# Gates, in_proj and ssm_out as 32x32 tiles in one block of a fused scan kernel

## The chip, the cores and the metric

The kernel runs on one NeuronCore of a Trainium2 chip. Its engines work side by side, each through its own list of instructions in order, and wait for one another by semaphores: TensorE (PE in the profile) multiplies matrices into PSUM, VectorE (DVE), ScalarE (ACT) and GpSimd (POOL) work element by element, SyncE (SP) issues DMAs. PSUM has eight banks, numbered 0 to 7 here, of 128 partitions by 512 float32. The metric is the device time of one launch in microseconds (us).

## The reference, cut to what matters

The input x is (4, 128, 96, 96) in float32. After a group norm it is read as four sequences of 9216 positions: along rows, rows reversed, along columns, columns reversed. Each goes through the same layer, and a matrix (fuse) joins the four results, which are added to x.

```python
t = _grouped1x1(x, in_proj_w, in_proj_b, 4)      # 4 groups: 128 -> 512 channels
u, gate = t[:, :256], t[:, 256:]
u = silu(u)
u = depthwise conv of u, 5 taps
s = ssm_in_w @ u                                 # 256 -> 32, as the next three
a = DMIN + (DMAX - DMIN) * sigmoid(ssm_delta_w @ u + b)
bb, cc = tanh(ssm_b_w @ u + b), tanh(ssm_c_w @ u + b)
prefix = cumsum(log(a))
hst = exp(prefix) * cumsum(bb * s * exp(-prefix))  # h = a*h + bb*s, step by step
u = u + ssm_out_w @ (cc * hst + ssm_d * s)       # 32 -> 256
u = _grouped1x1(u * sigmoid(gate), mix_w, mix_b, 4)
y = out_proj_w @ u                               # then fuse, over the four directions
```

All matrix products are float32.

## The kernel before

**Units and pairs.** mix, out_proj and fuse are multiplied into one matrix per direction ahead of the loop (`w_fin`). For each of the 4 images there are two phases, columns (V) and rows (H); a phase has 6 strips of 16 lines, a strip 4 parts p of 384 positions, and each part two units, s = 0 and s = 1: the forward and the reverse direction. The two units of a part make a pair; 4 x 2 x 6 x 4 = 192 pairs (NP = 24 a phase), and `pair(t)` runs once for each. k = t mod 4. A value that has 256 channels stands as two halves j of 128 partitions.

**What a pair does.** It works on several units at once, by a pipeline written out by hand. For pair t (units i = 2t), and for the pair n = t - 6 (units bi):

- `taps` (L636): the depthwise conv of channels 128 to 255, one tap after another in PSUM banks 0 and 1. Tap 0 (`first_tap`, L648) is ACT's, issued in the pair before; taps 1 to 4 (L650) are DVE's; the last writes u in SBUF.
- `conv` and `conv_less` (L610, L619): the conv of channels 0 to 127 on TensorE, by weights `band` and `less`. ACT copies the result to u (L629 as two copies, L631 as one).
- `proj` (L662): the four small projections of u into two banks; ACT takes them out (L687, L688, L693), POOL makes the scan's inputs (L695, L696).
- `scan` (L711): in pairs with k = 0 and 1, DVE runs the recurrence of a strip, in two parts (L722). `outputs` (L726): POOL makes cc\*h + d\*s of an older pair (L728, L729, L731); `scale_s` (L703) makes d\*s on ACT.
- `out_of` (L501), ssm_out: four matmuls of 32 rows by 128 columns for pair n, into banks 0 to 3. For most pairs ACT has first put u there (`under`, L509), and the matmul adds to it.
- `gate` (L487): four matmuls of 32 by 128, one for each s and j, and ACT's tanh of them (`sigmoids`, L514). Only the first 12 pairs of a phase need it: the other 12 mirror them, and use gates that were kept in SBUF or stored in DRAM (`kept`) and loaded again (`load_kept`, L534).
- `gating` (L582): DVE multiplies, v = (gate + 1) * (banks).
- `accumulate` (L742), below called W: a unit's v by `w_fin`, ACT's copy out of PSUM (L755, L757), POOL's addition to the result in SBUF (L774).
- `front` (L403), in_proj: for a strip four pairs ahead, 16 matmuls of 32 by 32 and four silus (L470). Only the first 3 strips of a phase need it; for the others the silus are stored and loaded again.

**Tiles of the array.** A matmul here uses part of TensorE's 128 x 128 array, as many rows as it has input partitions and as many columns as it has output partitions: `32*128` in the profile is 32 by 128. Matmuls on different parts run side by side. `mm` (L132) places one by its output partitions. Each float32 matmul shows as two instructions in the profile.

**The order on TensorE.** A pair without gates runs in_proj (if its strip is due), conv, W for both units, less, ssm_out, proj. A pair with gates runs conv, W of one unit, less, W of the other, gates and ssm_out mixed, proj. The first two pairs with gates in a phase have both. Each engine takes its instructions in the order in which the program names them, as the scheduler is switched off (`manual_schedule`, L1111).

**Banks.** 0 and 1 are shared by the taps and by ssm_out of s = 0, 2 and 3 are ssm_out's of s = 1. 4 to 7 go round between conv, W, proj, in_proj and gates (`plan`, L125).

**Statistics.** The group norm's statistics of the next image are made in pieces between other work (`stats_finish`, L180, a generator; each `yield` ends a piece).

Of the kernel before, what the change touches and what calls it, by code (L numbers as in the profile page):

```python
# [42 lines left out]
F32 = mybir.dt.float32  # L43
# [4 lines left out]
P = 128  # L48
# [8 lines left out]
R = 4  # L57
# [4 lines left out]
LAG = 6  # L62
# [5 lines left out]
def conv_preact_kernel(  # L68
# [111 lines left out]
    def stats_finish(b):  # L180
# [5 lines left out]

        mv = sp.tile([P, 2], F32, tag="mv", name=f"mv_{b}")
# [5 lines left out]
        nc.vector.tensor_copy(mean, pm[:, 0:1])  # L193
        dev = sp.tile([P, 1], F32, tag="dev", name=f"dev_{b}")
# [12 lines left out]
        nc.vector.tensor_scalar_add(var, pv[:, 0:2], GN_EPS)  # L207
        inv = sp.tile([P, 2], F32, tag="inv", name=f"inv_{b}")
        if b == b0:
            std = sp.tile([P, 2], F32, tag="err", name="std")  # L210
            nc.scalar.activation(std, var, AF.Sqrt)

            nc.scalar.activation(first_table, std[:, 0:1], AF.Silu)
            nc.vector.reciprocal(inv, std)
        else:
            bits = inv.bitcast(I32)
            nc.vector.tensor_single_scalar(bits, var.bitcast(I32), 1, ALU.logical_shift_right)
            nc.vector.tensor_scalar(bits, bits, -1.0, float(0x5F3759DF), ALU.mult, ALU.add)
            err = sp.tile([P, 2], F32, tag="err", name=f"err_{b}")
            for turn in range(3):  # L220
                if turn:
                    yield
                nc.gpsimd.tensor_mul(err, inv, inv)
# [3 lines left out]
        yield  # L227
        wns = sp.tile([P, 2, P], F32, tag="wn", name=f"wn_{b}")
# [16 lines left out]
        else:  # L245
# [3 lines left out]
            nc.vector.tensor_copy(shift, pb[:, 0:1])  # L249
            nc.vector.tensor_scalar_mul(spread, gmask, shift)  # L250
# [4 lines left out]
            nc.vector.tensor_sub(bn[:, 4:8], b_in[:, 4:8], pq[:, 0:4])  # L255
        nc.vector.tensor_scalar_mul(bn[:, 2:4], bn[:, 2:4], 0.5)
# [42 lines left out]

    b0 = phases[0][0]  # L300
# [7 lines left out]
    w_out_fuse = load(fuse, "fuse")  # L308
# [11 lines left out]
    w_mix = w_out_fuse[:, HID + 4 * P :].rearrange("p (j c) -> p j c", j=2)  # L320
# [140 lines left out]
    def in_proj(step, g, s, j, bk):  # L461
        wn = stats[units[step * UB]["b"]][0]
        r = slice(64 * s + 32 * j, 64 * s + 32 * j + 32)
        for c in range(4):
            m, q = (c, g) if j else (g, R - 1 - c if s else c)
            mm(bank(bk), c, wn[r, s, 32 * m : 32 * m + 32], x_in[s][r, q, :], True, True)

    def silu(step, g, s, j, bk):
# [3 lines left out]
            bank(bk)[:, : N + 1],  # L472
            AF.Silu,
# [19 lines left out]

    turning = (6, 0, 2)
# [11 lines left out]

    seeded = set()

    def under(bi, s):  # L509

        seeded.add(bi)
        nc.scalar.copy(psum[:, ssm(bi, s) : ssm(bi, s) + 2, :N], us[bi][:, s])  # L512

# [68 lines left out]
    def gating(bi, s):  # L582
# [3 lines left out]
        if m is None:  # L586
            g = gates[bi // 2 % 2][:, s]
        else:
            g = old_gates.get(bi // 2, gates[m % 2])[:, 1 - s, :, ::-1]
# [29 lines left out]
    def conv_less(i, banks):  # L619
# [10 lines left out]
        else:  # L630
            nc.scalar.copy(us[i][:, :, 0, :], psum[:, b0 : b0 + 2, :N])  # L631

# [291 lines left out]

    def tail():
# [90 lines left out]
    def start():  # L1016
        w_of = wp.tile([P, 4, 2, P], F32, name="w_of")

# [92 lines left out]
    with tc.manual_schedule(  # L1111
# [5 lines left out]
        for t in range(NU // 2):  # L1117
            pair(t)
        tail()
# [81 lines left out]
```

## Time and profile before

| | |
|---|---|
| median of 3 runs | 1811.15 us (1810.45 to 1817.87) |
| profiled execution, first to last instruction | 1812.7 us |
| TensorE busy | 1788.9 us, 99% |
| ACT busy | 1567.0 us, 86% |
| DVE busy | 1446.5 us, 80% |
| POOL busy | 1432.0 us, 79% |
| granted TensorE clock | 0.998 of full |

The time of the profiled execution is its span. A row of a view in order of time gives start and length in us, engine, line of the kernel, operation, the tile written and the tiles read, their sizes and, after x, how many instructions are merged in it. A row of stretches gives, for the time between two points, the busy time of each engine. A row of groups gives, after the bar, the sum of busy time in us, the mean duration of one in ns, then the idle time before them. Where a name stands behind an arrow in square brackets, the engine had waited, and the named one ended it.

### The profile page before, as it was taken

How to read it: one execution, taken by the hardware profiler on the slowest of the kernel's cores; microseconds unless marked ns; L12 is line 12 of the kernel's file. 1: busy time of each engine (PE TensorE's matmuls, PEld its weight loads, DVE VectorE, ACT ScalarE, POOL GpSimd, SP SyncE). 2: the span in 40 equal slices, each digit the busy share in tenths (PEclk: the TensorE clock that was granted, in tenths of full speed). 3: DMA queues.
4: the chain of work that ended last, by engine and by line, in shares of the span. 5: the costliest groups of instructions: out<-in, count | busy, mean ns of one | idle time of the engine just before them, and what ended most of it. 6: DMA issues, size and time to landing. Idle time of an engine off the chain costs nothing.

```text
span 1812.7 us, 56970 instructions
## 1 busy us (share of the span) xinstructions
PE 1788.9 (99%) x24090; PEld 645.3 (36%) x24090; DVE 1446.5 (80%) x1462; ACT 1567.0 (86%) x2750; POOL 1432.0 (79%) x1477
## 2 busy tenths in 40 slices
PE   6999999999999999999999999999999999999998
PEld 3333333333333333333333333333333333333333
DVE  5888878887888887877788888787877878777886
ACT  4988888998888888898988888889888888889975
POOL 3587887778778888788877888778778788887876
PEclk9999999999999999999999999999999999999999
DMA  7655463444975466344696447443477734645434
GB/s 229 183 184 196 149 185 117 163 145 142 305 246 188 159 177 204 102 145 141 204 306 225 159 161 211 138 146 119 160 232 223 249 118 150 192 122 176 148 112 175
DMA packets 148047, 321.17 MB, mean 177 GB/s; under 512 B 14160, under 2 KB 115920, under 8 KB 147792
## 3 DMA queue, kind: packets, MB, share of 16 engines
q1 hardware_dynamic: 147648, 317.48, 54.4%
q8 instruction: 190, 3.11, 0.7%
q14 instruction: 65, 0.53, 0.1%
q10 hardware_dynamic: 144, 0.04, 0.0%
HBM read 185.21 MB, written 132.25 MB: 175 GB/s over the span
## 4 chain that ended last, share of the span: by engine, by line
PE 95%; DMA 2%; DVE 2%; ACT 1%; issue 0%; SPq 0%; DVEq 0%
PE psum L134 82%; PE psum L504 8%; PE psum L491 5%; DVE psum L650 1%; DMA x_in<-in_xs 1%; DMA xs<-in_xr 1%; DMA acc<-in_xr 0%; DVE u L597 0%; DVE u L650 0%; ACT psum L512 0%; PE psum L1035 0%; ACT u L631 0%; SPq L296 0%; ACT ys L757 0%; DVE bn L387 0%
## 5 line engine op out<-in xcount | busy, mean ns | idle before, releaser
L650 DVE SCALAR_TENSOR_TENSOR psum<-sil,small,psum 128x768 f32<-128x768 f32 x576 | 589.0, 1023 | 28.4 <-ACT psum L648 3.4
L597 DVE SCALAR_TENSOR_TENSOR u<-gate,psum 128x768 f32<-128x768 f32 x376 | 350.0, 953 | 273.4 <-ACT u L629 119.0
L134 PE MATMUL psum<-u,w_fin 128*32 128x384 f32 (+1 forms) x6192 | 551.1, 485 | 1.6 <-ACT ys L755 1.2
L134 PE MATMUL psum<-u,main 128*32 128x384 f32 x6144 | 534.7, 489 | 1.5 <-DVE u L650 1.4
L774 POOL TENSOR_TENSOR acc<-ys,acc 128x384 f32<-128x384 f32 x375 | 411.6, 1119 | 24.0 <-ACT ys L757 7.9
L728 POOL TENSOR_TENSOR t<-t,t 64x384 f32<-64x384 f32 (+1 forms) x192 | 237.7, 1238 | 156.9 <-DVE t L722 73.2
L134 PEld LDWEIGHTS psum<-u,w_fin 128*32 128x32 f32 x6192 | 189.3, 109 | 319.6 <-issue 215.3
L134 PEld LDWEIGHTS psum<-u,main 128*32 128x32 f32 x6144 | 181.9, 109 | 324.7 <-issue 197.2
L512 ACT COPY psum<-u 128x768 f32<-128x768 f32 x352 | 277.3, 801 | 17.5 <-DVE u L650 11.5
L134 PE MATMUL psum<-sil,band 128*32 128x384 f32 x3072 | 285.1, 488 | 0.0
L695 POOL TENSOR_SCALAR t<-tm 64x384 f32<-64x384 f32 x191 | 176.9, 926 | 117.3 <-ACT tm L687 97.9
L729 POOL TENSOR_TENSOR t<-t,t 64x384 f32<-64x384 f32 (+1 forms) x192 | 249.1, 1297 | 15.0
L504 PE MATMUL psum<-t,main 32*128 32x384 f32 x1536 | 238.6, 513 | 1.3 <-ACT psum L512 0.6
L648 ACT ACTIVATE psum<-sil,small 128x768 f32<-128x768 f32 x191 | 173.7, 909 | 56.2 <-DVE u L597 48.0
L521 ACT ACTIVATE gate<-psum,bnorm 128x384 f32<-128x384 f32 x384 | 192.2, 584 | 26.5 <-PE psum L491 25.5
L696 POOL TENSOR_TENSOR t<-t,tm 64x384 f32<-64x384 f32 x192 | 195.3, 1017 | 15.3
L650 DVE SCALAR_TENSOR_TENSOR u<-sil,small,psum 128x768 f32<-128x768 f32 x192 | 194.9, 1015 | 7.8
L470 ACT ACTIVATE sil<-psum,bnorm 128x385 f32<-128x385 f32 x384 | 192.6, 585 | 7.1 <-PE psum L134 4.8
L134 PE MATMUL psum<-sil,less 64*32 64x384 f32 x3072 | 168.1, 495 | 0.0
L491 PE MATMUL psum<-x_in,wn 32*128 32x384 f32 x768 | 157.3, 527 | 0.0
L134 PEld LDWEIGHTS psum<-sil,band 128*32 128x32 f32 x3072 | 90.6, 109 | 169.2 <-issue 94.4
L731 POOL COPY t<-t 64x384 f32<-64x384 f32 x187 | 136.8, 731 | 11.9
(103 smaller groups left out, 1480.3 us busy)
## 6 DMA issues: line engine op xcount, KB each, us to landing
sil<-sil SPq DMA_DIRECT2D x128, 770.0 KB, 6.7
kept<-gate SPq DMA_DIRECT2D x80, 768.0 KB, 3.7
gate<-kept SPq DMA_DIRECT2D x76, 768.0 KB, 4.9
x_in<-in_xs SPq DMA_DIRECT2D x192, 96.2 KB, 2.5
out<-acc SPq DMA_DIRECT2D x48, 384.0 KB, 8.2
acc<-in_xr SPq DMA_DIRECT2D x39, 384.0 KB, 6.8
xs<-in_xr SPq DMA_DIRECT2D x72, 192.0 KB, 5.7
x_in<-in_xs SPq DMA_DIRECT2D x46, 192.5 KB, 3.5
```

The costliest lines, as they stand in the source:

```text
L134: nc.tensor.matmul(o[r, : rhs.shape[-1]], lhsT, rhs, start=start, stop=stop, skip_group_check=True)
L470: nc.scalar.activation(sils[step][:, s, j, g, :], bank(bk)[:, : N + 1], AF.Silu, bias=bn[:, 1:2] if j else bn[:, 4 + g : 5 + g],)
L491: nc.tensor.matmul(bank(to)[:, :N], stats[un["b"]][0][r, s, :], x_in[s][r, q, off : off + N], start=True, stop=True)
L504: nc.tensor.matmul(bank(ssm(bi, s) + j)[:, :N], w_so[r, bass.ts(j, P)], z[r, :], start=bi not in seeded, stop=True, skip_group_check=True)
L512: nc.scalar.copy(psum[:, ssm(bi, s) : ssm(bi, s) + 2, :N], us[bi][:, s])
L521: nc.scalar.activation(gv[:, s, j, :], bank(to[2 * s + j])[:, :N], AF.Tanh, bias=bn[:, 2 + j : 3 + j], scale=0.5,)
L597: nc.vector.scalar_tensor_tensor(v, g, 1.0, pz, ALU.add, ALU.mult)
L650: nc.vector.scalar_tensor_tensor(us[i][:, :, 1, :] if k == K - 1 else part, src, w_tap[:, k : k + 1], part, ALU.mult, ALU.add,)
L696: nc.gpsimd.tensor_mul(ta[0:64, p, :], tb[0:64, :], tm[0:64, :])
L728: engine.tensor_mul(ta[0:64, p, r], tb[64:P, r], ta[64:P, p, r])
L729: engine.tensor_add(tb[0:64, r], ta[0:64, p, r], tb[0:64, r])
L774: adder.tensor_add(part, y, part)
```

## The change

Pairs 0 to 7 run as before; from pair 8 on a new function, `pair_of_tiles`, takes the place of `pair`.

- ssm_out, gates and in_proj are all made of 32 x 32 matmuls: `out_tile` and `gate_tile` split the former 32 x 128 matmuls in four by columns, `in_proj_tile` is the former one. They stand in one block, in two halves of 16: the first has in_proj or gates of j = 1 and ssm_out of s = 0, the second in_proj or gates of j = 0 and ssm_out of s = 1. Their results go to banks `db`, 0 and 1, then `cb`, 2 and 3.
- The order on TensorE is W of both units, conv, less, block, proj. `cb` (conv's and less's) and `db` (W's and proj's) are banks 4, 5 and 6, 7 and change places from pair to pair.
- A gate is made one pair before its use. The gates of the first three pairs of a phase are made seven pairs before, in pairs 17 to 19 of the phase before, which have no gates or in_proj of their own; they go through a tile `shared` to DRAM and are loaded again. `shared` is the SBUF that held weights used only at the start. Pair 8 makes two sets of gates.
- Of the four silus or tanhs the two of j = 0 become one instruction over two banks.
- u's half j = 0 is copied from `cb` in two instructions: both on ACT for k below 2, one on ACT and one on DVE otherwise.
- `under` is used in every pair, so the additions of L596 fall away; `scale_s` comes one pair later; in pairs with k = 1 `outputs` comes after less; the pieces of `stats_finish` are cut smaller and stand between the taps.

```diff
...
     def stats_finish(b):
...
+        if b != b0:
+            yield
         mv = sp.tile([P, 2], F32, tag="mv", name=f"mv_{b}")
         nc.vector.bn_aggr(mv, stats[b].rearrange("p c s -> p (c s)"))
         yield
...
         nc.vector.tensor_copy(mean, pm[:, 0:1])
+        if b != b0:
+            yield
...
+    rp = ctx.enter_context(tc.tile_pool(name="shared", bufs=1))
+
+    def shared():
+        return rp.tile([P, 16 * P], F32, tag="shared", name="shared")
...
     def in_proj(step, g, s, j, bk):
+        for c in range(4):
+            in_proj_tile(step, g, s, j, bk, c)
+
+    def in_proj_tile(step, g, s, j, bk, c):
         wn = stats[units[step * UB]["b"]][0]
         r = slice(64 * s + 32 * j, 64 * s + 32 * j + 32)
-        for c in range(4):
-            m, q = (c, g) if j else (g, R - 1 - c if s else c)
-            mm(bank(bk), c, wn[r, s, 32 * m : 32 * m + 32], x_in[s][r, q, :], True, True)
+        m, q = (c, g) if j else (g, R - 1 - c if s else c)
+        mm(bank(bk), c, wn[r, s, 32 * m : 32 * m + 32], x_in[s][r, q, :], True, True)
 
...
+    def silu_both(step, g, j, b0):
+        bn = stats[units[step * UB]["b"]][1]
+        nc.scalar.activation(
+            sils[step][:, :, j, g, :],
+            psum[:, b0 : b0 + 2, : N + 1],
             AF.Silu,
...
+    def gate_tile(n, s, j, to, c):
+        un = units[2 * n + s]
+        q, off = gate_at(un)
+        r = slice(64 * (1 - s) + 32 * j, 64 * (1 - s) + 32 * j + 32)
+        mm(bank(to), c, stats[un["b"]][0][r, s, bass.ts(c, 32)], x_in[s][r, q, off : off + N],
+           True, True)
...
+    def out_tile(bi, s, j, c):
+        r = slice(64 * j + 32 * s, 64 * j + 32 * s + 32)
+        mm(bank(ssm(bi, s) + j), c, w_so[r, bass.ds(j * P + 32 * c, 32)], tbs[bi][r, :], False, True)
...
+    def tile_of(n):
+        m = mirror(n)
+        return gates[((n % NP if m is None else m) + n // NP) % 2]
+
     def load_kept(n):
         m = mirror(n)
+        if n % NP < 3 and NP <= n < NU // 2:
+            nc.sync.dma_start(tile_of(n), kept[n // NP % 2][n % NP])
         if n < NU // 2 - R and m is not None and m < NP // 2 - 2:
-            old_gates[n] = gates[m % 2]
-            nc.sync.dma_start(old_gates[n], kept[n // NP % 2][m])
...
+    def less_both(i, banks):
+        step, p = units[i]["step"], units[i]["p"]
+        sil, k = blocks(step), less_of(p)
+        for g in range(4):
+            for s in range(2):
+                r = less_rows(s, p)
+                mm(bank(banks[s]), g, less[r, p, g, :], columns(step, sil[s][r, g, :], k), False, True)
...
+    def pair_of_tiles(t):
+        i, k, n, end = 2 * t, t % R, t - LAG, NU // 2
+        bi, last = 2 * n, t == end - 1
+        cb, db = ((4, 5), (6, 7))[:: 1 if t % 2 == 0 else -1]
+        late = (n - 1) % (NP * 2) == 0
+        step, g = divmod(t + R, R)
+        fronted, gated = fresh(step), None
+        if mirror(n + 1) is None and (n + 1) % NP > 2:
+            gated = n + 1
+            to = tile_of(gated)
+        elif t % NP in (17, 18, 19) and t + LAG + 1 < end:
+            gated = t + LAG + 1
+            to = shared()[:, : 4 * N].rearrange("p (s j n) -> p s j n", s=2, j=2)
+
+        if not fronted:
+            front(t + R, None)
+        for e in soon:
+            load_kept(e)
+        soon.clear()
+        if t < end - 2:
+            send()
+        if len(reload) == 4 and (k == 1 or late):
+            for b, r in reload:
+                nc.sync.dma_start(accf[:, r], xr[b, :, r])
+            reload.clear()
...
+        new_u(i)
+        taps(i, (1, 2))
+        piece = later and k > 1
+        if piece:
+            free[0] = SSM + 2
+            next(later[0], None)
+        taps(i, (3, 4))
+        if piece:
+            next(later[0], None)
+        under(bi, 1)
+        if t > LAG + 2:
+            scale_s(i - 4)
+        if k < 2:
+            scan(t // R - 1, k)
+        if k != 1:
+            outputs(i - 10)
+        for add in held:
+            add()
+        held.clear()
+        adds = [accumulate(waiting.pop(0), b, *((nc.vector, True) if last else ())) for b in db]
+        if late:
+            held.extend(adds)
+        else:
+            for add in adds:
+                add()
+
+        conv(i, cb)
+        under(bi, 0)
+        less_both(i, cb)
+        if k == 1:
+            outputs(i - 10)
+        stats_chunks(t)
+        for s, copy in enumerate((nc.scalar.copy, nc.scalar.copy if k < 2 else nc.vector.tensor_copy)):
+            copy(us[i][:, s, 0, :], bank(cb[s])[:, :N])
+
+        if fronted and g == 0:
+            sils[step] = wk.tile([P, 2, 2, 4, N + 1], F32, tag="sil", name=f"sil_{step}")
+        for j in (1, 0):
+            for c in range(4):
+                for s in range(2):
+                    if fronted:
+                        in_proj_tile(step, g, s, j, (cb, db)[j][s], c)
+                    elif gated is not None:
+                        gate_tile(gated, s, j, (cb, db)[j][s], c)
+                for e in range(2):
+                    out_tile(bi, 1 - j, e, c)
+
+        if fronted:
+            for s in range(2):
+                silu(step, g, s, 1, db[s])
+        elif gated is not None:
+            for s in range(2):
+                tanh_one(gated, to, s, 1, db[s])
+        gating(bi, 0)
+        first_tap(i + 2)
+        gating(bi, 1)
+        if fronted:
+            silu_both(step, g, 0, cb[0])
+            if step % NS == 0:
+                for j in range(2):
+                    edges(step, g, j, nc.gpsimd)
+            after_front(step, g)
+        elif gated is not None:
+            tanh_both(gated, to, 0, cb[0])
+            if gated % NP < NP // 2 - 2:
+                nc.sync.dma_start(kept[gated // NP % 2][gated % NP], to)
+            for s in range(2):
+                load_gate(2 * gated + s + UB)
+        if t % NP in (14, 15, 16, 17):
+            for s in range(2):
+                load_gate(2 * (t + 10) + s)
+        un = units[i]
+        if un["order"] == "V" and un["b"] + 1 < B and un["st"] == NS - 1 and k == R - 1:
+            later[:] = [stats_finish(un["b"] + 1)]
+        if t + 2 < end:
+            load_chunks(t + 2)
+        if k == 2 and not last:
+            soon.append(n + 2)
+        else:
+            load_kept(n + 2)
+        if last:
+            for s in range(2):
+                under(bi + 2, s)
+            outputs(i - 8, None)
+        proj(i, db, True)
+        if last:
+            scale_s(i - 2)
+        waiting.extend(units[bi : bi + 2])
+        if t >= end - 4:
+            load_last(t)
+        if n % (NP * 2) == 0:
...
-        for t in range(NU // 2):
+        for t in range(LAG + 2):
             pair(t)
+        for t in range(LAG + 2, NU // 2):
+            pair_of_tiles(t)
```

More of the change, by code (lines that the diff above doesn't have):

```diff
@@ L307, in conv_preact_kernel @@
     load_x([(0, 1), (1, 1), (2, 1), (3, 2), (5, 2), (7, 3), (10, 4), (14, 4), (18, 4), (22, 2)])
-    w_out_fuse = load(fuse, "fuse")
+    w_out_fuse = shared()
+    nc.sync.dma_start(w_out_fuse[:, 0 : 2 * HID + 4 * P], fuse)
     w_main = load(main, "main")
@@ L1016, in start @@
     def start():
-        w_of = wp.tile([P, 4, 2, P], F32, name="w_of")
         def filler(n):
```

43 lines of the change are left out of this document (40 added, 3 removed).

## The prediction

> **What bounds the kernel now.** I read the page's first part, then busy time by stretches, then TensorE alone in order of time, and last what stands between two of its blocks.
>
> ```profile
> PE 1788.9 (99%) x24090; PEld 645.3 (36%) x24090; DVE 1446.5 (80%) x1462; ACT 1567.0 (86%) x2750; POOL 1432.0 (79%) x1477
> ```
> ```profile
> core 0: us, PE busy (x) PEld busy (x) DVE busy (x) ACT busy (x) POOL busy (x), PEclk, DMA share, GB/s
> 199.74:209.00 9.26, 9.26 (x143) 3.12 (x136) 8.60 (x8) 8.18 (x16) 8.67 (x11) 1.00 0.82 229
> 115.64:124.75 9.11, 9.11 (x113) 3.38 (x112) 6.92 (x8) 8.17 (x15) 8.50 (x10) 1.00 0.59 197
> 90.90:1772.50 1681.60, 1679.67 (x22600) 599.58 (x22596) 1353.60 (x1329) 1483.95 (x2600) 1367.42 (x1386) 1.00 0.55 176
> ```
>
> TensorE never stops: a pair with in_proj takes 9.26 us, one with gates 9.11, and in both it is busy throughout. The last row runs from the conv of pair 8 to that of pair 191, the last, so over the 183 pairs that the change rewrites: 9.19 us each. ACT needs 8.2 us of a pair. A busy TensorE is not a full one, though; what the blocks cost shows in their starts. A pair with in_proj:
>
> ```profile
> 199.74 1.50 PE L134 MATMUL psum<-sil,band 128*32 128x384 f32 x16
> 201.06 2.76 PE L134 MATMUL psum<-u,w_fin 128*32 128x384 f32 x32
> 203.75 0.88 PE L134 MATMUL psum<-sil,less 64*32 64x384 f32 x16
> 204.56 0.93 PE L504 MATMUL psum<-t,main 32*128 32x384 f32 x8
> 205.41 2.79 PE L134 MATMUL psum<-u,main 128*32 128x384 f32 x32
> 208.13 0.94 PE L134 MATMUL psum<-x_in,wn 32*32 32x385 f32 x32
> 209.00 0.53 PE L134 MATMUL psum<-sil,band 128*32 128x384 f32 x4
> ```
>
> Part of a pair with gates, and one of the last pairs, which have neither:
>
> ```profile
> 119.53 1.47 PE L134 MATMUL psum<-u,w_fin 128*32 128x384 f32 x16
> 120.94 0.88 PE L134 MATMUL psum<-sil,less 64*32 64x384 f32 x16
> 121.74 1.50 PE L134 MATMUL psum<-u,w_fin 128*32 128x384 f32 x16
> ```
> ```profile
> 1738.79 1.47 PE L134 MATMUL psum<-sil,band 128*32 128x384 f32 x16
> 1740.08 2.76 PE L134 MATMUL psum<-u,w_fin 128*32 128x384 f32 x32
> ...
> 1743.58 0.93 PE L504 MATMUL psum<-t,main 32*128 32x384 f32 x8
> 1744.43 2.79 PE L134 MATMUL psum<-u,main 128*32 128x384 f32 x32
> 1747.04 1.47 PE L134 MATMUL psum<-sil,band 128*32 128x384 f32 x16
> ```
>
> Three things are to be seen. Eight matmuls of one shape followed by the same shape take 1.29 us (conv, 1738.79 to 1740.08), so four column tiles side by side take 0.645; before a block of another tile shape the same eight take 1.41 (119.53 to 120.94) and after one 1.32 (199.74): a change of shape costs 0.12 at the end of a block and 0.03 at the head of the next. Sixteen 32x32 tiles (in_proj) take 0.87 and four 32x128 ones (ssm_out) 0.85, each with a change of shape: either fills the array once. And each pair changes shape four times.
>
> **The change, part by part: the block.** Now each pair has one block of 32 tiles of 32x32: two sets of 16, each with eight of ssm_out and eight of in_proj or of gates, on sixteen different places of the array and with a bank of its own for each row of places. By the rows: 0.87 for the first set with the change of shape, 0.645 for the second, 1.52. Around it proj, both W and conv stand in a row in one shape: proj 2.61 (1744.43 to 1747.04), W 2 x 1.29 = 2.58, conv before less 1.41, less 0.80 (120.94 to 121.74). Sum 2.61 + 2.58 + 1.41 + 0.80 + 1.52 = 8.92. Of the 183 pairs, 177 are full (pairs 8 to 184), for the three that had neither gates nor in_proj now make early gates; six have ssm_out alone, 8.92 - 0.645 = 8.27. Pair 8 makes two sets of gates, about 1.0 more. That is 177 x 8.92 + 6 x 8.27 + 1.0 = 1629.4, against 1681.6: **52 us less, if nothing waits.**
>
> **What waits.** in_proj's second set writes the two banks from which u has just been copied, and the block now follows less at once; before, W or ssm_out and proj lay between. T is the block's start.
>
> ```profile
> 204.10 0.53 PE L134 MATMUL psum<-sil,less 64*32 64x384 f32 x8
> ...
> 204.72 0.86 ACT L629 COPY u<-psum 128x384 f32<-128x384 f32 x2 [0.31 <-PE psum L134]
> ```
> ```profile
> 49.99 0.80 ACT L631 COPY u<-psum 128x768 f32<-128x768 f32 x1
> ...
> 50.84 0.16 PEld L134 LDWEIGHTS psum<-u,main 128*32 128x32 f32 x8 [0.74 <-ACT u L631]
> ```
> ```profile
> 1744.64 0.95 DVE L597 SCALAR_TENSOR_TENSOR u<-gate,psum 128x768 f32<-128x768 f32 x1 [2.16 <-PE psum L504]
> ```
> ```profile
> L629 ACT COPY u<-psum 128x384 f32<-128x384 f32 x178 | 76.9, 486 | 17.2 <-PE psum L134 17.0
> L1031 DVE COPY w_of<-psum 128x256 f32<-128x256 f32 x1 | 0.4, 424 | 0.0
> L774 DVE TENSOR_TENSOR acc<-psum,acc 128x384 f32<-128x384 f32 x5 | 2.7, 547 | 0.0
> ```
>
> In the pair above, the block (ssm_out) starts at 204.56, less ends at 204.63 = T+0.07, and ACT's two copies run from 204.72 (T+0.16) to T+1.02. A waiting TensorE starts 0.05 after ACT's end (50.79 to 50.84); DVE starts 0.13 after TensorE's (ssm_out's end 1744.51 to 1744.64). The second set could start at T+0.03+0.645 = T+0.67.
> - In pairs of k below 2 (t mod 4) both copies are ACT's: the second set's second tile starts at 1.02 + 0.05 = 1.07, **0.40 late**. The wait stands at the head of TensorE's queue: ssm_out's tiles behind it wait as well, then proj, W and the next pair.
> - In the others DVE copies one half. No row shows it; ACT's own half is there at 0.16 + 0.49 + 0.05 = 0.70. DVE's is bounded below by 424 ns (256 columns) and above by 424 x 1.5 = 636; I take 547, DVE's reading of this very shape with one operand more. 0.07 + 0.13 + 0.55 + 0.05 = 0.80: **0.13 late**, bounds 0.00 and 0.22.
>
> Of pairs 8 to 184, 89 have k below 2 and 88 not: 89 x 0.40 + 88 x 0.13 = 47 us. In three of the six short pairs proj waits for the second copy: 1.07 - 0.87 = 0.20 each, 0.6. Sum: -52.2 + 47.0 + 0.6 = **-4.6 us**. The wait for u's copy takes back nearly all that the packing gives.
>
> **The other engines.** Against a pair of some 9.05 (k above 1) to 9.32 us:
>
> ```profile
> L650 DVE SCALAR_TENSOR_TENSOR psum<-sil,small,psum 128x768 f32<-128x768 f32 x576 | 589.0, 1023 | 28.4 <-ACT psum L648 3.4
> L648 ACT ACTIVATE psum<-sil,small 128x768 f32<-128x768 f32 x191 | 173.7, 909 | 56.2 <-DVE u L597 48.0
> ```
> ```profile
> 198.94 0.47 ACT L688 COPY t<-psum 64x384 f32<-64x384 f32 x1
> 199.44 0.58 ACT L693 ACTIVATE t<-psum,small 64x384 f32<-64x384 f32 x1
> ...
> 202.08 1.54 ACT L512 COPY psum<-u 128x768 f32<-128x768 f32 x2
> 203.56 0.85 ACT L757 COPY ys<-psum 128x384 f32<-128x384 f32 x2
> ...
> 205.46 0.62 ACT L705 ACTIVATE t<-t,small 64x384 f32<-64x384 f32 x1
> ```
>
> The first set's ssm_out tiles need u put into PSUM (`under`), the last of ACT's run after proj: 0.50 + 0.60 + 1.54 + 0.85 + 0.62 = 4.11, from 0.07 after proj's end. TensorE is 2.58 + 1.41 + 0.80 - 0.18 (2.79 - 2.61, the last matmul's tail) = 4.61 away from the block by then: 0.43 to spare. The ring of four taps (4 x 1.02), `under` 0.80, the first set about 0.95, gating 0.95 and first tap 0.91, with five hops of 0.05 to 0.13, is 8.1 to 8.3: it fits; DVE's busiest pair has 8.60 in the stretches above, scan included. The wide silu or tanh saves ACT about 0.2 a pair and the 30 adds that DVE loses are off the path: nothing. W now comes ahead of conv and needs gating done; it starts 2.6 after proj, gating ends about 3 after T: hidden by proj. The re-spaced statistics put a pair between TensorE's small products and DVE's answers; without that cover TensorE would stand ahead of W for about two taps. The loads and stores that `after_front` issues move from a pair's head to its middle and stand on SP behind what was issued at the head; their tiles are needed pairs later. The early gates add 21 loads of kept gates (their stores existed before, in a later pair), issued two pairs ahead of use as the others are; ACT's next early tanh waits for the store of the pair before, which has some 6 us until then. POOL keeps its instructions. All this I cost at nothing.
>
> **The rivals.**
> 1. *The wait is hidden*: ssm_out's tiles pass the waiting ones, or the copies are done in the first set's time. Time: 1811.15 - 52 = 1759. For it: 0.03 and 0.13 are all that is missing for the copies that two engines share. Against it: where TensorE waited for a copy (50.84), nothing behind passed. Chance 0.15. [...]
> 2. *ACT comes late (slower)*. If nothing in ACT's run overlapped and each of its seven steps cost a hop of 0.05 to 0.1, the run would be 4.6 to 4.95 and the 0.43 would be gone; from there `under` holds the block and u's copies behind it, each 0.1 us late costing 18 us. At 0.15 late: +27, 1833. For it: ACT is the busiest beside TensorE; against it, rows in which such steps overlap. Chance 0.20.
> 3. *The tiles don't run as sixteen*: completions or feeding go one after another. By the rows, 12 more tiles (in_proj's 16 against ssm_out's 4) cost 0.02 us, so 16 to 24 more cost 0.04, +7 us. If in_proj's and ssm_out's tiles shared the array only in turn, each pair would pay a set more, 0.645 x 177 = 114: 1921. Chance 0.10, between the two. [...]
>
> **How the numbers follow.** The profile's span, 1812.7, lies 1.5 above the median of the runs, 1811.15, from which I count: 1811.15 - 4.6 = **1806.5 us**, chance 0.55. Its own range: with 0.00 for DVE and 0.35 for ACT (no time to wake) the waits are 31 us, 1790; with DVE's upper bound, 0.13 instead of 0.05 to wake and 0.03 for a first load that nothing hides they are 0.33 and 0.51, 74 us, 1834. Cases lie outside on both sides; the range is 1785 to 1836, with about 0.1 left out below and above. 0.5% is about what a measurement tells from no change: 1802 and 1820. Of the forecast's 0.55, 0.23 lies below, 0.25 within, 0.07 above; rival 1 is faster; of rival 2, 0.03 is within and 0.17 slower; rival 3 is slower. Faster 0.38, same 0.28, slower 0.34.
>
> **What would show it.** Right: pairs of two lengths by k, near 9.05 and 9.32; conv, W and proj without a change of shape; the block's second set starting 0.8 and 1.07 after its first; TensorE's waits led by the copy of u on ACT. Wrong: blocks of 1.52 in all pairs (rival 1); TensorE waiting for `under`, or u's copies starting later than 0.1 after less (rival 2); a set of over 0.7 with nothing to wait for (rival 3).

## The result, and the profile after

The changed kernel takes 1843.13 us (median of 4 runs, 1842.83 to 1845.45), the kernel before 1811.14 in the same comparison: a ratio of 1.0174, with an interval of 1.0156 to 1.0192. It is 1.7% slower. The forecast was 1806.5, a little faster, and the time lies outside its range. The profiled execution has a span of 1843.6 us, 0.5 above the median.

First the totals of the page, then busy time by stretches (from conv to conv): a pair with k = 0, one with k = 2, and the 183 pairs from the conv of pair 8 to that of pair 191.

```profile
PE 1815.0 (98%) x30762; PEld 679.5 (37%) x30762; DVE 1462.7 (79%) x1526; ACT 1537.8 (83%) x2607; POOL 1478.9 (80%) x1477
```
```profile
core 0: us, PE busy (x) PEld busy (x) DVE busy (x) ACT busy (x) POOL busy (x), PEclk, DMA share, GB/s
660.35:669.68 9.33, 9.33 (x165) 3.36 (x161) 8.15 (x8) 8.15 (x15) 8.53 (x10) 1.00 0.50 165
679.01:688.30 9.29, 9.29 (x164) 3.52 (x160) 7.35 (x10) 7.76 (x14) 8.69 (x11) 1.00 0.93 275
97.44:1805.73 1708.29, 1703.03 (x29213) 634.03 (x29209) 1365.43 (x1388) 1452.05 (x2452) 1410.96 (x1384) 1.00 0.59 182
```

The pairs hold the loss: 1708.29 us against 1681.60 before. Pairs with k below 2 take 9.33 (forecast 9.32), the others 9.30 (forecast 9.05; the row's 9.29 is a rounded end). The forecast seems to hold for the first half and to fail by 0.25 in the second. That reading is wrong, as the runs below show.

The block of the pair with k = 2, in order of time. A row is two tiles, `x2`; each tile runs two passes, so it comes twice.

```profile
681.22 0.51 PE L134 MATMUL psum<-x_in,wn 32*32 32x385 f32 x2
681.23 0.51 PE L134 MATMUL psum<-t,main 32*32 32x384 f32 x2
...
681.36 0.55 PE L134 MATMUL psum<-t,main 32*32 32x384 f32 x2
681.38 0.48 ACT L1063 COPY u<-psum 128x384 f32<-128x384 f32 x1 [0.56 <-PE psum L134]
681.49 0.56 DVE L1063 COPY u<-psum 128x384 f32<-128x384 f32 x1 [1.32 <-PE psum L134]
681.56 0.49 PE L134 MATMUL psum<-x_in,wn 32*32 32x385 f32 x2
...
681.91 0.69 PE L134 MATMUL psum<-x_in,wn 32*32 32x385 f32 x2
682.11 0.51 PE L134 MATMUL psum<-t,main 32*32 32x384 f32 x2
682.13 0.52 PE L134 MATMUL psum<-x_in,wn 32*32 32x385 f32 x2
682.16 0.52 PE L134 MATMUL psum<-t,main 32*32 32x384 f32 x2
682.20 0.52 PE L134 MATMUL psum<-x_in,wn 32*32 32x385 f32 x2
...
682.69 0.50 PE L134 MATMUL psum<-t,main 32*32 32x384 f32 x2
683.12 1.18 PE L134 MATMUL psum<-u,main 128*32 128x384 f32 x12
```

T is 681.22, the block's start. The first set stands on the array at once: its first ten tiles start 6.7 ns apart, the next five 16.7 ns apart, and the last is there at T+0.19. The second passes follow at T+0.35. The second set begins at 681.91, T+0.69, as forecast (0.67); its second tile comes 0.19 later, at T+0.885, and from there two tiles take 33 ns, 16.7 a tile. proj begins at T+1.905; the block was forecast at 1.52 and a wait of 0.13. The copy of VectorE ends at 682.05, T+0.83.

Two more places lost time. Pair 8 makes an extra set of gates ahead of W, and the first W writes the banks of that set, so it waits for the first of the two wide tanh that take the set out; ACT began them only after the results of proj. This W then ran at less than full clock (two rows in order of time, and a stretch with the granted clock in its third column from the right):

```profile
92.19 1.69 ACT L563 ACTIVATE gate<-psum,bnorm 128x768 f32<-128x768 f32 x2
93.14 4.48 PE L134 MATMUL psum<-u,w_fin 128*32 128x384 f32 x32 [1.78 <-ACT gate L563]
```
```profile
94.00:98.00 4.00, 4.00 (x36) 1.41 (x32) 2.66 (x2) 1.50 (x3) 3.86 (x3) 0.61 0.69 246
```

And near two of the three changes of image TensorE stands still a few times without a wait that the profile could name:

```profile
513.83 2.42 PE L134 MATMUL psum<-u,main 128*32 128x384 f32 x25 [0.60 <-issue]
```
```profile
498.32:528.30 29.98, 29.26 (x484) 10.75 (x480) 23.45 (x24) 24.54 (x42) 21.98 (x22) 1.00 0.89 289
949.44:981.47 32.03, 29.27 (x485) 10.47 (x481) 23.32 (x24) 24.54 (x42) 23.03 (x22) 1.00 0.84 273
```

These are three pairs each (51 to 53, 99 to 101), which should take 27.96, so 6.1 us are lost in them. Pair 57 takes 11.00, 1.7 us too long, behind a gate's tanh. Near the third change of image, pair 147, no pair is long.

### The profile page after: what moved, and what is told of

It reads as the page before. It is cut to its first block, busy times and chain, and to the rows that moved or that the text cites. A ratio compares the mean times of both kernels' runs of the same rounds, so it can differ in the third digit from the quotient of the medians.

```text
span 1843.6 us, 70463 instructions
## 1 busy us (share of the span) xinstructions
PE 1815.0 (98%) x30762; PEld 679.5 (37%) x30762; DVE 1462.7 (79%) x1526; ACT 1537.8 (83%) x2607; POOL 1478.9 (80%) x1477
## 3 DMA queue, kind: packets, MB, share of 16 engines
q8 instruction: 243, 3.98, 0.9%
## 4 chain that ended last, share of the span: by engine, by line
PE 96%; DVE 1%; DMA 1%; ACT 1%; issue 1%; SPq 0%; DVEq 0%
PE psum L134 95%; DMA xs<-in_xr 1%; DVE psum L720 0%; DMA acc<-in_xr 0%; PE psum L1216 0%; PE psum L541 0%; DVE u L659 0%; DVE t L792 0%; DVE u L720 0%; PE psum L521 0%; ACT psum L718 0%; SPq L307 0%; ACT psum L553 0%; PE psum L1223 0%; PE psum L1231 0%
## 5 line engine op out<-in xcount | busy, mean ns | idle before, releaser
L134 PE MATMUL psum<-u,w_fin 128*32 128x384 f32 (+1 forms) x6192 | 535.7, 485 | 5.4 <-ACT gate L563 3.2
L844 POOL TENSOR_TENSOR acc<-ys,acc 128x384 f32<-128x384 f32 x375 | 451.3, 1226 | 74.1 <-ACT ys L825 32.4
L134 PE MATMUL psum<-x_in,wn 32*32 32x385 f32 (+1 forms) x6080 | 361.5, 493 | 0.0
L134 PE MATMUL psum<-t,main 32*32 32x384 f32 x5888 | 351.0, 492 | 0.3 <-ACT psum L553 0.2
L553 ACT COPY psum<-u 128x768 f32<-128x768 f32 x380 | 308.0, 811 | 9.8 <-DVE u L659 3.8
L134 PEld LDWEIGHTS psum<-u,w_fin 128*32 128x32 f32 x6192 | 202.4, 110 | 297.2 <-issue 245.0
L799 POOL TENSOR_TENSOR t<-t,t 64x384 f32<-64x384 f32 (+1 forms) x192 | 295.2, 1537 | 15.1
L798 POOL TENSOR_TENSOR t<-t,t 64x384 f32<-64x384 f32 (+1 forms) x192 | 234.4, 1221 | 20.7 <-DVE t L792 4.5
L1063 ACT COPY u<-psum 128x384 f32<-128x384 f32 x276 | 123.2, 481 | 97.9 <-PE psum L134 97.9
L134 PEld LDWEIGHTS psum<-x_in,wn 32*32 32x32 f32 x6080 | 123.8, 103 | 212.1 <-ACT psum L553 108.8
L1063 DVE COPY u<-psum 128x384 f32<-128x384 f32 x92 | 51.3, 558 | 155.0 <-PE psum L134 154.1
```

The costliest lines, as they stand in the source:

```text
L134: nc.tensor.matmul(o[r, : rhs.shape[-1]], lhsT, rhs, start=start, stop=stop, skip_group_check=True)
L798: engine.tensor_mul(ta[0:64, p, r], tb[64:P, r], ta[64:P, p, r])
L799: engine.tensor_add(tb[0:64, r], ta[0:64, p, r], tb[0:64, r])
L844: adder.tensor_add(part, y, part)
L1063: copy(us[i][:, s, 0, :], bank(cb[s])[:, :N])
```

## The experiments

The edits are shown shortened: dots and words in square brackets stand for code. A ratio is to the kernel before, with its interval behind it.

**Theory A**, from the rows above: VectorE's copy frees the waiting tile 0.19 sooner than ACT's second copy does, but the tiles queued behind it then come slowly, at 16.7 ns; wait and slow feeding together are the excess, and without the wait the pair is the dense one of the prediction, 8.92. Rival B: the wait counts as the prediction says, and something else is too long. Rival C: the block, or the order, is slow by itself.

### Both copies on ACT

```diff
-for s, copy in enumerate((nc.scalar.copy, nc.scalar.copy if k < 2 else nc.vector.tensor_copy)):
+for s, copy in enumerate((nc.scalar.copy, nc.scalar.copy)):
```

> Both copies of u on ACT in every pair, so VectorE has none. Theory A (feeding): in pairs of k 2 and 3 the tile that waits for VectorE's copy starts 0.19 earlier than the one that waits for ACT's second copy (T+0.887 against T+1.075), but the tiles behind it then come at 16.7 ns instead of 7, so all that VectorE's copy gives is 0.03 a pair (9.30 against 9.33). Without it: 88 x 0.03 = 2.6 us more than the changed kernel, 1846. Rival B (the terms of the prediction hold for the wait, and the 0.25 us that these pairs are too long come from something beside the copy): the copy is still worth 0.40 - 0.13 = 0.27 a pair, 88 x 0.27 = 24 us more, 1867.

Measured: 1836.57, ratio to before 1.0164 (1.0136 to 1.0193). A pair with k = 2:

```profile
671.35:680.68 9.33, 9.33 (x164) 3.37 (x160) 6.92 (x9) 8.15 (x15) 8.66 (x11) 1.00 0.90 278
```

All pairs now take 9.33, so VectorE's copy is worth 0.03 a pair, as A said and B did not. The whole is no longer than the changed kernel, though, but 4 to 7 us shorter (1840.47 and 1843.13 in its two comparisons): the stalls at pairs 51 to 57 and 99 to 101 (7.8 us together in the changed kernel) are not there.

### The waiting tiles left out

```diff
-for s in range(2):
+for s in range(2) if j else ():
     if fronted:
         in_proj_tile(step, g, s, j, (cb, db)[j][s], c)
```

> Leaves out the eight in_proj or gate tiles of the block's second set, which write the banks that u is copied from (half of in_proj and of the gates is not computed; silu and tanh still read the banks). Nothing in the block waits for u's copy any more; the set's eight ssm_out tiles remain, on rows of their own. Theory A: the wait and the slow feeding behind it are the whole excess, so the pair is the dense one of the prediction, 8.92: 177 x (9.315 - 8.92) = 70 us less than the changed kernel, 1773. Rival C (the mixed block or the new order is itself slower than the rows of before said, or ACT's run holds it): pairs stay above 9.2, 1820 or more.

Measured: 1798.31, ratio 0.9941 (0.9920 to 0.9961). The pair, and its block in order of time:

```profile
566.40:575.51 9.11, 9.11 (x148) 3.43 (x144) 8.02 (x8) 8.14 (x15) 8.44 (x7) 1.00 0.31 110
```
```profile
632.43 0.51 PE L134 MATMUL psum<-x_in,wn 32*32 32x384 f32 x2
...
632.91 1.30 PE L134 MATMUL psum<-t,main 32*32 32x384 f32 x18
634.18 1.18 PE L134 MATMUL psum<-u,main 128*32 128x384 f32 x12
```

The time is under that of the kernel before because work is left out. 9.11, not 8.92: A falls. Nothing in this block waits for u, eight tiles fewer stand in it, and it takes 1.75 us instead of 1.52 (1.72 in most pairs). Tile by tile, the second set again starts with one tile at T+0.68, the next at T+0.864, and then one every 16.7 ns.

### The waiting tiles last

```diff
-for j in (1, 0):
-    for c in range(4):
-        [in_proj or gates of j] ; [ssm_out of s = 1 - j]
+for c in range(4):
+    [in_proj or gates of j = 1] ; [ssm_out of s = 0]
+for c in range(4):
+    [ssm_out of s = 1]
+for c in range(4):
+    [in_proj or gates of j = 0]
```

> The second set in another order: its eight ssm_out tiles first, the eight that wait for u's copy last. Theory A: behind the wait stand 8 tiles instead of 15. In pairs of k 2 and 3, where they come at 16.7 ns, that takes away 7 x 16.7 = 0.12 us, in the others, at 7 ns, 0.05: 88 x 0.12 + 89 x 0.05 = 15 us less than the changed kernel, 1828. Rival B (the wait alone sets the end of the block, whatever stands behind it): 1843, within 3 us.

Measured: 1834.92, ratio 1.0144 (1.0124 to 1.0164). The pairs take 9.30 whatever k is; with k = 2:

```profile
679.44:688.74 9.30, 9.30 (x164) 3.62 (x160) 7.39 (x10) 7.77 (x14) 8.64 (x11) 1.00 0.90 274
```
```profile
681.65 0.51 PE L134 MATMUL psum<-x_in,wn 32*32 32x385 f32 x2
...
682.14 0.98 PE L134 MATMUL psum<-t,main 32*32 32x384 f32 x10
682.63 0.50 PE L134 MATMUL psum<-x_in,wn 32*32 32x385 f32 x1
...
683.56 0.53 PE L134 MATMUL psum<-u,main 128*32 128x384 f32 x4
```

Here the eight ssm_out tiles, which wait for nothing, start at T+0.67 to T+0.97, with the same gap and the same slow pace; the first that needs u's copy comes at T+0.98, long after both copies (T+0.64, T+0.83). Nothing waits, and proj still begins at T+1.906. So neither A nor B: the block of 32 tiles takes 1.905 us with no wait in it at all. Where ACT makes both copies, the wait adds 0.03.

### W between less and the block

```diff
-cb, db = ((4, 5), (6, 7))[:: 1 if t % 2 == 0 else -1]
+cb, db = (4, 5), (6, 7)
...
-adds = [accumulate(waiting.pop(0), b, ...) for b in db]
-conv(i, cb); under(bi, 0); less_both(i, cb)
-[two copies of u]
+w_of_one(db[0])
+conv(i, cb); under(bi, 0); less_both(i, cb)
+nc.scalar.copy(us[i][:, :, 0, :], psum[:, cb[0] : cb[0] + 2, :N])
+w_of_one(db[1])
...
-[block: j = 1 into db, j = 0 into cb] ; proj(i, db, True)
+[block: j = 1 into cb, j = 0 into db] ; proj(i, cb, True)
```

> The W of one unit between less and the block, the banks fixed (conv and proj 4 and 5, W 6 and 7), the block's first set into 4 and 5, the second into 6 and 7; one copy of u for both halves on ACT. u's copy has 1.3 us of W as its cover. By the prediction's rows: 8.92 and one more change of shape (0.12 + 0.03) make 9.07 a pair, 177 x (9.315 - 9.07) = 43 us less than the changed kernel, 1800, and less than the kernel before. Rival D (ACT takes proj's results out too late for a conv that comes after one W instead of two): conv waits 0.1 to 0.3 a pair, 1818 to 1853.

Measured: 1855.77, ratio 1.0252 (1.0237 to 1.0268); pairs of 9.44. In order of time:

```profile
586.25 0.51 PE L134 MATMUL psum<-x_in,wn 32*32 32x384 f32 x2
...
586.94 0.68 PE L134 MATMUL psum<-x_in,wn 32*32 32x384 f32 x2
587.13 0.52 PE L134 MATMUL psum<-t,main 32*32 32x384 f32 x2
587.17 0.52 PE L134 MATMUL psum<-x_in,wn 32*32 32x384 f32 x2
...
588.16 0.53 PE L134 MATMUL psum<-u,main 128*32 128x384 f32 x4
```

u's copy has all of W as cover. What the second set waits for instead, ACT's copy of that W, ends at T+0.62, before the set could start. The block still takes 588.16 - 586.25 = 1.91 with the same gap and pace. From conv to block 3.64 pass, which is 1.41 + 0.80 + 1.29 + 0.15 = 3.65: conv, less and W are as forecast, so rival D (ACT late for conv) falls, and the new order costs its change of shape, 0.15.

**Theory F**, then: instructions come to TensorE too slowly for 32 small tiles in a row. A tile is four instructions (two weight loads, two matmuls); the page's instruction queue bears that out, as it moved 3.98 MB against 3.11 before, 65 bytes for each of the 13,344 further matmuls and weight loads. By the theory some ten tiles' worth stand ready at the head of the block and go at 6.7 ns a tile; what is beyond comes at 16.7 ns a tile, 4.2 ns an instruction, after a gap of 0.19. Rival G: a second set on places already used loses 0.19, whatever its tiles.

### Wide tiles in pairs with gates

```diff
+for j in (1, 0) if not fronted else ():
+    for s in range(2) if gated is not None else ():
+        gate_wide(gated, s, j, (cb, db)[j][s])   # 32x128
+    for e in range(2):
+        out_of(bi, 1 - j, e)                     # 32x128
-for j in (1, 0):
+for j in (1, 0) if fronted else ():
     [the block of 32x32 tiles]
```

> In pairs with gates (and in the six short ones) the block is made of 32x128 tiles, 8 instead of 32, in the same two sets and the same order; pairs with in_proj stay as they are. Theory F (instructions reach TensorE too slowly for 32 tiles: the block of 32x32 takes 1.905 us by itself, and the wait for u lies under it): with 8 tiles the second set is there at T+0.68, and now the wait for u shows: T+0.88 in pairs of k 2 and 3, so 8.92 + 0.20 = 9.12 a pair, T+1.07 in the others, 9.31. In_proj pairs 9.30 and 9.33 as before. Some 44 pairs x 0.18 + 44 x 0.02 = 9 us less than the changed kernel. Rival G (a second set on places that the first has used loses 0.19 us, whatever its tiles): the same times in this kernel, but the second tile of the second set at T+0.87 where nothing waits. Rival C (the order, not the tiles, costs the time): 9.30 and 9.33 everywhere.

Measured: 1831.53, ratio 1.0116 (1.0096 to 1.0135), 9 us less than the changed kernel in the same comparison (1840.47). Gate pairs take 9.13 (k = 2, 3) and 9.32, in_proj pairs 9.30 and 9.33. C falls: in pairs with k = 2 and 3 the same order with eight tiles is 0.17 faster. Only now the wait for u shows, and with it VectorE's copy is worth its 0.19.

### The same with W between

The change of the last experiment, made in the kernel with W between less and the block.

> W of one unit between less and the block, and in pairs with gates 32x128 tiles. Nothing waits for u here. Theory F: the eight tiles take 1.52 us, so gate pairs are 8.92 + 0.15 for one more change of shape = 9.07, in_proj pairs with their 32 tiles 9.44 as in the run with 32x32 tiles everywhere: 88 x 0.37 = 33 us less than that run, 1823. Rival G: 0.19 is lost between the sets, 9.26, 88 x 0.18 = 16 us less, 1840. Rival C: 9.44 everywhere, 1856.

Measured: 1826.09, ratio 1.0095 (1.0078 to 1.0112), 30 us less than with 32x32 tiles everywhere. A gate pair and an in_proj pair of the same run:

```profile
573.79:582.90 9.11, 9.11 (x117) 3.37 (x113) 8.02 (x8) 8.11 (x14) 8.57 (x7) 1.00 0.31 108
646.66:656.09 9.43, 9.43 (x164) 3.45 (x160) 8.26 (x8) 8.11 (x14) 8.89 (x10) 1.00 0.52 170
```

```profile
577.42 0.59 PE L535 MATMUL psum<-x_in,wn 32*128 32x384 f32 x2
...
579.00 0.53 PE L134 MATMUL psum<-u,main 128*32 128x384 f32 x4
```

The in_proj pairs are the control: 32 tiles, 9.43; eight tiles, 9.11. The block of eight takes 1.58 (1.52 forecast; its second set's weights are loaded once ACT's copy of W, over at T+0.62, is seen at T+0.67). Tile by tile the second set starts at T+0.752 and the next tile 7 ns later: G falls too.

### Sixteen tiles of 32x64

```diff
-gate_wide(gated, s, j, ...) ; out_of(bi, 1 - j, e)
+for h in range(2):
+    gate_half(gated, s, j, ..., h) ; out_half(bi, 1 - j, e, h)   # 32x64
```

> As the run with W between and wide tiles, but in pairs with gates (and the short ones) the block is of 16 tiles of 32x64, two sets of eight, in place of eight of 32x128. There is no wait for u in it. Theory F (a queue of some ten tiles' instructions stands ready, and what is beyond it comes at 4.2 ns an instruction, 16.7 ns a tile): eight tiles of a set are within the queue, so the block is as with wide tiles, gate pairs 9.11, 1826. If every tile costs, 8 tiles 9.11 and 32 tiles 9.44 make 9.22 for 16, 88 x 0.11 = 10 us more, 1836. If any tile narrower than the array pays the whole price: 9.44, 1855.

Measured: 1827.77, ratio 1.0101 (1.0079 to 1.0123).

```profile
573.81:582.93 9.12, 9.10 (x132) 3.17 (x128) 8.01 (x8) 8.10 (x14) 8.58 (x7) 1.00 0.31 109
```
```profile
577.45 0.54 PE L532 MATMUL psum<-x_in,wn 32*64 32x384 f32 x2
...
579.04 0.53 PE L134 MATMUL psum<-u,main 128*32 128x384 f32 x4
```

Sixteen tiles cost what eight do (block 1.59 and 1.58); the 24 of the run without the waiting tiles took 1.72, and 32 take 1.905. It is neither each tile nor their being narrow; it is the number beyond the first sixteen.

What holds the further tiles back is less clear. In the three runs in which nothing holds the second set (without the waiting tiles, with them last, with W between) every full block breaks at the same place: sixteen tiles and one of the second set go, and the next comes 0.17 to 0.19 later. Slow delivery alone doesn't give this. From T+0.21, the first set's last weight load, to T+0.68 nearly half a microsecond passes, in which at 4.2 ns an instruction about 110 could have come, more than the 64 of the second set. So something kept them back until the first set was done; what it was, no run shows. Counted in instructions, the block of 64 (sixteen tiles) takes 0.01 us more than that of 32 (eight tiles), the block of 128 takes 0.31 more than that of 64, and the break comes after 68.

### Wide ssm_out beside small in_proj tiles

```diff
 for j in (1, 0):
+    for e in range(2) if fronted else ():
+        out_of(bi, 1 - j, e)                     # 32x128
     for c in range(4):
         [in_proj tiles of 32x32]
-        [ssm_out tiles of 32x32]
+        [ssm_out tiles of 32x32, in pairs with gates only]
```

> In pairs with in_proj ssm_out runs as two 32x128 tiles in each set, beside the set's eight 32x32 tiles of in_proj: 20 tiles instead of 32 on the same places. Gate pairs stay. Theory F, if tiles of two shapes run side by side: 80 instructions instead of 128, the block between 1.52 and 1.75, the wait for u still at T+0.88 and T+1.07: in_proj pairs 9.12 to 9.15 (k 2 and 3) and 9.31, 44 x 0.17 + 44 x 0.02 = 8 us less than the changed kernel. If each change of shape empties the array, four parts of 0.65 to 0.85 us one after another, about 3.0 instead of 1.905: 88 x 1.1 = 97 us more, 1940.

Measured: 1954.59, ratio 1.0793 (1.0777 to 1.0809); in_proj pairs of 10.69.

```profile
691.49 0.91 PE L541 MATMUL psum<-t,main 32*128 32x384 f32 x4
692.33 0.88 PE L134 MATMUL psum<-x_in,wn 32*32 32x385 f32 x16
693.14 0.91 PE L541 MATMUL psum<-t,main 32*128 32x384 f32 x4
693.98 0.88 PE L134 MATMUL psum<-x_in,wn 32*32 32x385 f32 x16
694.79 0.53 PE L134 MATMUL psum<-u,main 128*32 128x384 f32 x4
```

Here tiles of two shapes do not run side by side, even on rows of their own: four parts, each 0.81 to 0.84, follow one another (3.30 in all). in_proj and ssm_out were seen side by side only with one shape for both (1.905 with 32x32); that much of the change is needed.

### The changed kernel once more, and without the reload

> The changed kernel once more, to see whether its five stalls in the middle of the run (pairs 51 to 57 and 99 to 101, 9 us together) belong to it. If they do, 1843 and pairs of 10 to 11.6 us in the same places; if they come with one execution and not with another, 1834 to 1843, and the pairs elsewhere as before, 9.33 and 9.30.

Measured: 1840.47, ratio 1.0166 (1.0150 to 1.0181). The long pairs are the same, 51, 52, 57 and 99 to 101, with other lengths (10.23 where it was 10.48, 9.95 where it was 11.59) and one more, 48; 4.9 us instead of 7.8; pair 53 takes its usual time. They belong to the kernel; their size changes from execution to execution.

```diff
 if len(reload) == 4 and (k == 1 or late):
-    for b, r in reload:
-        nc.sync.dma_start(accf[:, r], xr[b, :, r])
     reload.clear()
```

> The changed kernel without the loads that put the next image into the accumulator (four of 384 KB at each change of image; images 1 to 3 are then added onto the one before). Theory S (TensorE's stalls near pairs 51 to 57 and 99 to 101, which name no wait, are instructions that come late behind the image's transfers): without these loads the pairs 51 to 53 and 99 to 101 take 9.3 to 9.5 like the rest, 5 to 8 us less than the changed kernel, 1834 to 1837. Rival (they come from VectorE's copy of u or from another transfer): they stay, 1841 to 1843.

Measured: 1835.63, ratio 1.0134 (1.0118 to 1.0149). The same two groups of three pairs:

```profile
493.13:521.11 27.98, 27.98 (x485) 10.27 (x480) 23.34 (x24) 24.31 (x42) 22.62 (x22) 1.00 0.81 252
942.14:970.10 27.96, 27.96 (x484) 10.25 (x480) 23.34 (x24) 24.31 (x42) 22.63 (x22) 1.00 0.80 252
```

27.98 and 27.96 instead of 29.98 and 32.03: without the image's loads the stalls are gone, in this one execution. Pair 57 stays at 10.89; there a scan (L792) shows 4.9 us instead of 2.1, and the gate's tanh is late. In the kernels that copy u on ACT alone no scan takes over 2.7 us; the cause is open. That the stalls are late instructions is not shown, nor that the loads are always needed for them. Nor is it settled what u's copy has to do with it: in the four variants above that copy u on ACT alone no pair takes over 9.71; of the five kernels that use VectorE too and reload the image, three (the changed one, the one with the waiting tiles last and the one with wide gates) stall in these pairs and two (the one with tiles left out and the mixed one) do not.

### A version after this

```diff
-[block of 32 tiles of 32x32]
+for s in range(2):
+    [in_proj or gates of j = 1, 32x128, into db[s]]
+[ssm_out of s = 0, 32x128]
+[ssm_out of s = 1, eight tiles of 32x32]
+for s in range(2):
+    [in_proj or gates of j = 0, s, four tiles of 32x32, into cb[s]]
```

> The changed kernel with another block: a first set of four 32x128 tiles (in_proj or gates of j = 1, whose four small tiles share their input, and ssm_out of s = 0), then a second of sixteen 32x32 tiles, ssm_out of s = 1 first, then in_proj or gates of j = 0, s = 0 and s = 1. Copies of u as in the changed kernel. Theory F: the first set takes 0.844 with its change of shape (row of the mixed run), the second 0.87 like in_proj's sixteen before: block 1.71, and no set of small tiles follows another, so the queue does not run dry. u's copy by VectorE (T+0.88) lies under it, by ACT (T+1.07) it is 0.06 late. Pairs 7.40 + 1.71 = 9.11 to 9.13 (k 2 and 3) and 9.18: 177 x 0.16 = 28 us less than the changed kernel, 1813. Rival (the four wide tiles and the small ones empty the queue just as well, or u's copy holds the second set): pairs stay at 9.30, 1841.

Measured: 1822.43, ratio 1.0056 (1.0043 to 1.0069). Pairs of 9.20 to 9.21 (k = 2, 3) and mostly 9.25: F's direction, but 0.07 to 0.09 short; the block takes 1.81 (k = 2, 3), not 1.71. Where nothing waits (k = 2, 3), thirteen of the second set's sixteen tiles come at 6.7 ns and the last three 33 to 43 ns apart. With the four wide tiles ahead of them that makes seventeen tiles again before the pace breaks, though the shapes are others.

```diff
-for s, copy in enumerate(...):
-    copy(us[i][:, s, 0, :], bank(cb[s])[:, :N])
+nc.scalar.copy(us[i][:, :, 0, :], psum[:, cb[0] : cb[0] + 2, :N])
```

> The same block, and u copied by one instruction of ACT in all pairs (0.80 instead of 2 x 0.48, over at T+0.96). The small tiles that wait for it are there at T+1.01 to T+1.07, where the last of them would come at about T+1.03 unhindered: pairs of 9.15 to 9.18 for all k. VectorE copies nothing; if its copy is what brings the stalls at pairs 51 to 57 and 99 to 101 (none was seen in the three kernels in which ACT copies alone), they stay away, 8 us less: 1805 to 1810, level with the kernel before or a little faster. Else 1813 to 1818.

Measured: 1822.54, ratio 1.0057 (1.0043 to 1.0071); pairs of 9.23 for all k, no stall. It is above all that was expected: the stalls stayed away as they should, but the block takes 1.84, and the pair is 0.05 to 0.08 longer than forecast.

```profile
578.23:587.46 9.23, 9.23 (x141) 3.36 (x137) 8.01 (x8) 8.05 (x14) 8.15 (x7) 1.00 0.31 109
```

Both win back about 1.2% of the changed kernel's 1.7% and stay 0.6% behind the kernel before. No version here that does the whole work beats that one.

## Why the prediction was wrong, step by step

The profiled execution lies 1843.6 - (1806.5 + 1.5) = 35.6 us above the forecast's sum on the profile's scale. Of these 22.9 are the pairs (89 x 0.01 + 88 x 0.25), 7.8 the seven long pairs (6.1 at two changes of image, 1.7 in pair 57), and 3.6 pair 8; the rest is small change.

- **The dense parts**: right. conv to block takes 2.21 (1.41 + 0.80), proj, W, W and conv stand in one shape, and a change of shape costs what the rows said, down to the 0.15 of the order with W between.
- **"By the rows: 0.87 for the first set with the change of shape, 0.645 for the second, 1.52."** This is the step that failed. The first half held: sixteen tiles stand on the array at once and the second set begins at T+0.69. But 0.645 for a second set came from tiles of which there are four to a set, and no row of before had two sets of sixteen in a row. Measured: 1.905, 0.385 more, 68 us over 177 pairs, and that with nothing to wait for: after seventeen tiles a gap of 0.17 to 0.19, then 16.7 ns a tile. What keeps the further tiles back is open. The gain of 52 us was never there; the dense pair is 9.30, longer than before's 9.19.
- **"What waits"**: each piece was right, and it did not matter. ACT's copy ends at T+1.02 and the tile starts at T+1.07, as forecast, and none behind it passes; VectorE's takes 558 ns (forecast 547), starts 0.07 later than forecast and frees its tile at T+0.885 instead of T+0.80. But the wait lies under a block that takes 1.905 anyway, and costs 0.03 instead of 0.40. That pairs with k below 2 came out at 9.33 against 9.32 is two errors that cancel: 0.385 too little for the block and 0.37 too much for the wait. In pairs with k above 1 the forecast had only 0.13 of wait to cancel against it, and the error showed.

```profile
L1063 ACT COPY u<-psum 128x384 f32<-128x384 f32 x276 | 123.2, 481 | 97.9 <-PE psum L134 97.9
L1063 DVE COPY u<-psum 128x384 f32<-128x384 f32 x92 | 51.3, 558 | 155.0 <-PE psum L134 154.1 <-ACT psum L553 0.9
```

- **Rival 1**, the wait is hidden: true, in a way it didn't think of, and worth nothing, since what hides it is longer than it.
- **Rival 2**, ACT late: false. `under`'s last copy ends 0.40 before the block, where 0.43 was forecast.
- **Rival 3**, feeding: the nearest to what the runs showed, at the wrong price. It was priced by one row with sixteen tiles in the block (12 more than four, 0.02 us): +7 us. The price is not proportional: 0.01 at sixteen tiles (1.59 against the 1.58 of eight), 0.13 at 24, 0.31 at 32.
- **"About 1.0 more" for pair 8**: 3.6 too little. The forecast counted the extra set's matmuls, but not that W writes the banks of that set and waits for its tanh: the matmuls end at 91.35, ACT begins the first wide tanh at 92.19, and W starts at 93.14 (1.78 us of idle). In this execution a W at a granted clock of 0.61 followed (4.48 us instead of 2.79); where the clock held, as in the kernel with both copies on ACT, the pair was 1.7 us shorter.
- **Loads and stores at nothing**: 6.1 us wrong in this execution, in the stalls at two changes of image, which were gone in the run without the reload.

## What to carry to other kernels

Packing more tiles into a block was paid for here: with W between less and the block, the same products took 1.58 us as eight tiles and 1.91 as 32. So count how many stand in one run of short tiles, since here seventeen tiles, 68 instructions, went before the pace broke and the rest came slower (16.7 ns a tile, after a gap of 0.17 to 0.19 us), and take the widest tile whose columns share their input. A duration that was read on one set of small tiles need not hold for a second one behind it: sixteen took 0.87 us in the kernel before, two sets of sixteen took 1.905. And two terms that were never seen apart can cancel: an agreement in one half of the pairs was no evidence for either.

## What the runs showed of the hardware that was not expected

- 32x32 tiles of two passes started 6.7 ns apart at the head of a block (the first ten in the changed kernel). With two sets in a row a gap of 0.17 to 0.19 us came after seventeen tiles, and from there they started 16.7 ns apart (4.2 ns an instruction). Blocks took 1.58 (eight tiles of 32x128), 1.59 (sixteen of 32x64), 1.72 (24 of 32x32) and 1.905 (32 of 32x32).
- Tiles of 32x128 and of 32x32 on separate rows of the array ran one shape after the other: 3.30 us, where 32x32 tiles alone took 1.905 for the same products.
- The idle of 1.8 us on TensorE ahead of pair 8 was followed by a granted clock of 0.61 over 4 us in the changed kernel (94.00 to 98.00), and by one of 1.00 over the 4 us behind it in the run with both copies on ACT (90 to 94) and in the one with W between and wide tiles (91 to 95).
